# First attention of a fused block on Trainium2: the causal mask in 32-row matmuls, projections split around the last flips, weights loaded in another order

## The chip, the cores and the metric

The kernel runs on one core of one Trainium2 chip, as one launch. Its time is the device time of that core in microseconds. TensorE (PE) does the matmuls and transposes, VectorE (DVE), ScalarE (ACT) and GpSimd (POOL) the elementwise work. SyncE (SP) and POOL issue the DMAs.

## The reference, cut to what matters

A block over `x` of 8 batches x 128 positions x 512: a per-batch weight, a causal attention, a second attention with a paged cache, and a low-rank feed-forward. The change touches only the first two lines:

```python
h = einsum('bsi,boi->bso', x, weight[adapter_ids])       # one 512x512 weight per batch
q = (h @ wq)  # 32 heads of 16;   k, v = h @ wk, h @ wv   # 8 heads of 16, each for 4 query heads
scores = where(causal, q @ k.T * 0.25, lowest)
x = x + (softmax(scores) @ v) @ wo
x = x + ffn(attention_with_paged_cache(x))               # 32 heads of 128, untouched
```

## The kernel before, in words

The program is written in an order by hand: each engine executes its instructions in the order in which the code below emits them, and waits on semaphores where an operand is not ready. Tiles come from pools with a fixed number of buffers; a new tile waits until the oldest of its tag is free.

**Set-up.** SP's queue loads, in this order: `ids`, the first `x` (`load_x(0)`), `lens`, `freq`, `x1`, the weights of keys, values and queries of the first attention (`wk_sb`, `wv_sb` of 256 KB, `wq_sb` of 1 MB), four small page tables, the output weights (`wo_sb`, 1 MB), two more `x`, and small constants. SP has eight semaphores for these loads in turn, so a ninth load waits until the first has landed. POOL makes an identity and a causal mask, then gathers the weights of batch 0 and batch 1 from HBM (`gather_w`, four indirect DMAs of 256 KB each, rows given by `idx_w`).

**Per batch.** `flip_x` transposes `x` (PE, then a copy by ACT); `condition` multiplies with the gathered weights (`hp`, L498) and a copy makes `hT`; `project_kv` and `project_q` give keys, values and queries; `keep_k`, `keep_v` (ACT) and `keep_q` (DVE) move them out of PSUM.

**Per half-batch k (16 of them), 16 query heads.** `scores1` fills four PSUM banks j. First the mask goes in (L562): for each bank a matmul of the identity (weights, 128x128 bf16) with the mask (128x512 bf16). Then the products of queries and keys are added (L572): for each bank two matmuls that use only 32 of the 128 rows, rows 32j to 32j+31. DVE takes the maxima (`nm`), ACT the exponentials (`exps1`), DVE the sums and POOL the division (`divide1`). In the *next* step, `flip_p` transposes the probabilities in four portions j (PE, L615), each copied out as `pT` by DVE or ACT, and `values1` (L634) multiplies them with the values. `p_tp`, the PSUM pool of all transposes, has two buffers, and so has `p_mm`, that of the projections and products.

The main loop interleaves these. In even k: scores, `condition` of the next batch, flips 0 and 1 of the last step, divisions, keys and values of the next batch, flips 2 and 3 (copied by ACT), `values1`. In odd k: scores, output projection `out_proj1` of the batch before (L650), flips 0 and 1, divisions, queries of the next batch, flips 2 (ACT) and 3 (DVE), `flip_x`, `values1`. After the 16 half-batches come 64 units of the second attention and the feed-forward, where the change touches nothing.

Of the kernel before, what the change touches and what calls it, by code (L numbers as in the profile page):

```python
# [10 lines left out]

F32 = mybir.dt.float32
BF16 = mybir.dt.bfloat16
# [6 lines left out]
P = 128  # L20
# [21 lines left out]
def block_kernel(  # L42
# [47 lines left out]
    def tile_a(shape, name):  # L90
        return both.tile(shape, F32, tag="a", name=name, bufs=12)
# [184 lines left out]
    with (  # L276
# [9 lines left out]
        def load_x(b):  # L286
            if b < B:
                xss[b] = p1.tile([P, DM], F32, tag="xs", name=f"xs_{b}", bufs=4)
                nc.sync.dma_start(out=xss[b][:], in_=x[b])

        def gather_w(b):
            if b < B:
# [30 lines left out]
        ]  # L323
        for v in vpad:
            nc.vector.memset(v[:], 0.0)
        identb = p1w.tile([P, P], BF16, tag="identb", name="identb")
        nc.vector.tensor_copy(identb[:], ident[:])
        causal_f = both.tile([P, P], F32, tag="ka", name="causal_f")
        make_causal_mask(nc, causal_f[:], NEG)
        causal = p1w.tile([P, 4, P], BF16, tag="causal", name="causal")  # L330
        for n in range(4):
            nc.vector.tensor_copy(causal[:, n, :], causal_f[:])
        for c in range(KC):
            nc.vector.tensor_scalar(
                idx_w[:, c, :], ids[:], float(DM), iota_pf[:, c : c + 1], ALU.mult, ALU.add
            )
        gather_w(0)
        load_x(1)
        for sb, src in ((wk_sb, wk1), (wv_sb, wv1), (wq_sb, wq1)):
            nc.sync.dma_start(out=sb[:], in_=src.rearrange("(c p) e -> p c e", p=P))  # L340
        gather_w(1)

        pages = p1w.tile([P, B * NBLK], I32, tag="pages", name="pages")
        for n in range(4):
            nc.sync.dma_start(
                out=pages[n * PSIZE : (n + 1) * PSIZE, :],
                in_=table[n : n + 1].rearrange("n b k -> n (b k)").to_broadcast([PSIZE, B * NBLK]),
            )
        nc.sync.dma_start(out=wo_sb[:], in_=wo1.rearrange("(r p) e -> p r e", p=P))
        load_x(2)  # L350
        load_x(3)
        wn = [both.tile([P, D2], F32, tag="kb", name=f"wn_{n}") for n in range(2)]
        nc.sync.dma_start(out=wn[0][:], in_=qn_w.unsqueeze(0).to_broadcast([P, D2]))
        nc.sync.dma_start(out=wn[1][:], in_=kn_w.unsqueeze(0).to_broadcast([P, D2]))
# [17 lines left out]
        def angles():  # L372

            fr = p1.tile([P, B, D2 // 2], F32, tag="pT", name="ang_f", bufs=5)
            kf = p1.tile([P, B, D2 // 2], F32, tag="pT", name="ang_k", bufs=5)

            for n, key in enumerate(("sin", "cos")):
                trig[key] = x1T[B - 1 - n][:].rearrange("p c (h d) -> p (c h) d", d=HALF)
            pos = p1.tile([P, B], F32, tag="pos", name="pos", bufs=1)
            nc.vector.tensor_copy(lens_f[:], lens[:])  # L380
            nc.vector.tensor_scalar(pos[:], lens_f[:], iota_pf[:, :1], None, ALU.add)
            for b in range(B):
                nc.vector.tensor_scalar(fr[:, b, :], freq[:], pos[:, b : b + 1], None, ALU.mult)
            nc.vector.tensor_scalar(kf[:], fr[:], 1.0 / (2 * PI), ROUND, ALU.mult, ALU.add)
            nc.vector.tensor_scalar(kf[:], kf[:], ROUND, None, ALU.subtract)
            for part in (TWO_PI_1, TWO_PI_2, TWO_PI_3):
                nc.vector.scalar_tensor_tensor(fr[:], kf[:], -part, fr[:], ALU.mult, ALU.add)
            nc.vector.tensor_scalar(kf[:], fr[:], PI / 2, -2 * PI, ALU.is_gt, ALU.mult)
            nc.vector.scalar_tensor_tensor(kf[:], fr[:], PI / 2, kf[:], ALU.add, ALU.add)
            for a, t in ((fr, trig["sin"]), (kf, trig["cos"])):  # L390
                nc.vector.tensor_scalar(a[:], a[:], PI_IN, -PI_IN, ALU.min, ALU.max)
                nc.scalar.activation(t, a[:], AF.Sin)

        def tables(n):
            for here, there in ((lo, hi), (hi, lo)):
# [95 lines left out]
        def condition(b):  # L491
            hp = p_mm.tile([P, KC, S], F32, tag="mm", name=f"hp_{b}")
            parts = [(oc, c) for oc in range(KC) for c in range(KC)]
            if b == 0:

                parts.sort(key=lambda part: part[1])
            for n, (oc, c) in enumerate(parts):
                nc.tensor.matmul(  # L498
                    hp[:, oc, :],
                    cws[b][c][:, oc * P : (oc + 1) * P],  # L500
                    xT[b][:, c, :],
                    start=(n == 0 if b == 0 else c == 0),
                    stop=(n == KC * KC - 1 if b == 0 else c == KC - 1),
                )
            hT[b] = both.tile([P, KC, S], F32, tag="vg", name=f"hT_{b}", bufs=4)
            nc.vector.tensor_copy(hT[b][:], hp[:])

        def project_q(b):
            ps = p_mm.tile([P, REP, S], F32, tag="mm", name=f"qp1_{b}")
            for r in range(REP):  # L510
                for c in range(KC):
                    nc.tensor.matmul(  # L512
                        ps[:, r, :],
                        wq_sb[:, c, r * P : (r + 1) * P],
                        hT[b][:, c, :],
                        start=(c == 0),
                        stop=(c == KC - 1),
                    )
            return ps

        def keep_q(b, ps):
            qT[b] = p1.tile([P, REP, S], F32, tag="qT1", name=f"qT1_{b}")
            nc.vector.tensor_scalar(qT[b][:], ps[:], SCALE1, None, ALU.mult)

        def project_kv(b):
            ps = p_mm.tile([P, 2, P], F32, tag="mm", name=f"kvp1_{b}")
            for c in range(KC):
                nc.tensor.matmul(
                    ps[:, 0, :], wk_sb[:, c, :], hT[b][:, c, :], start=(c == 0), stop=(c == KC - 1)
                )  # L530
            for c in range(KC):
                nc.tensor.matmul(
                    ps[:, 1, :], hT[b][:, c, :], wv_sb[:, c, :], start=(c == 0), stop=(c == KC - 1)
                )
            return ps

        def keep_k(b, ps):
            kbd[b] = p1.tile([P, 2, S], F32, tag="kbd", name=f"kbd_{b}")
# [16 lines left out]
        def scores1(k):  # L555
            b, hb = divmod(k, 2)
            h = H[k]
            h["sc"] = [
                p_sc.tile([P, 2, 4 * S], F32, tag="sc", name=f"sc1_{k}_{n}") for n in range(2)
            ]  # L560
            for j in range(4):
                nc.tensor.matmul(  # L562
                    h["sc"][j // 2][:, j % 2, :],
                    identb[:],
                    causal[:].rearrange("p n t -> p (n t)"),
                    start=True,
                    stop=False,
                )
            for rr in range(2):
                for j in range(4):  # L570
                    rows = slice(32 * j, 32 * j + 32)
                    nc.tensor.matmul(  # L572
                        h["sc"][j // 2][:, j % 2, rr * 2 * S : (rr + 1) * 2 * S],
                        qT[b][rows, 2 * hb + rr, :],
                        kbd[b][rows].rearrange("p h t -> p (h t)"),
                        start=False,
                        stop=(rr == 1),
                    )
            h["nm"] = p1.tile([P, 2, 8], F32, tag="nm1", name=f"nm1_{k}")
            for n in range(2):  # L580
                nc.vector.tensor_reduce(
                    h["nm"][:, n, :],
                    h["sc"][n][:].rearrange("p j (h t) -> p (j h) t", t=S),
                    AX.X,
                    ALU.max,
                    negate=True,
                )
            h["pr"] = []
# [72 lines left out]
        by_vector, by_scalar = nc.vector.tensor_copy, nc.scalar.copy  # L661

        flip_x(0)
        angles()
        condition(0)
        flip_x(1)
        kv = project_kv(0)
        keep_k(0, kv)
        keep_v(0, kv)
        keep_q(0, project_q(0))  # L670
        gather_w(2)

        for k in range(2 * B + 1):
# [4 lines left out]
            if hb == 0:  # L678
# [17 lines left out]
                    divide1(k, 0)  # L696
                    divide1(k, 1)
                if more:
                    kv = project_kv(b + 1)
                if k == 2 * B:  # L700
                    merge_b(0)
                if k:
                    flip_p(last, 2, by_scalar)
                    flip_p(last, 3, by_scalar)
                if more:
                    keep_k(b + 1, kv)
                if k == 2 * B:
                    merge_b(1)
# [9 lines left out]
            else:  # L718
# [6 lines left out]
                divide1(k, 0)  # L725
                divide1(k, 1)
                if more:
                    ps = project_q(b + 1)
                    keep_q(b + 1, ps)
                else:  # L730
                    for c in range(KC):
                        q_matmul(0, c)
                    for part in q_turn(0):
                        part()
                    for c in range(KC):
                        kv_matmul(0, c)
                flip_p(last, 2, by_scalar)
                flip_p(last, 3, by_vector)
                if not more:
                    kv_turn(0)  # L740
                    norms(0)
                if b + 2 < B:
# [360 lines left out]
```

## Time and profile before

| | us |
|---|---|
| median of 3 runs (1441.12 to 1443.71) | 1442.05 |
| the profiled execution, its time | 1443.16 |
| the profiled execution, its span | 1441.4 |
| PE busy in the span | 1404.8 (97%) |
| DVE, ACT, POOL busy | 932.7, 652.6, 564.3 |
| first attention, mask matmuls (L562), first to last start | 25.8 to 207.0 |
| one pair of half-batches (58.83 to 83.41) | 24.58 |

Busy time of PE is the union of its matmuls, whose ends are modelled; a matmul that has been started counts as busy although the next one may already be waiting. About a quarter of the mask's records (16 of 64) are missing from the trace. The distance between the starts of two groups is therefore the safer reading than the busy time of one.

### The profile page before, as it was taken

The numbers are of one execution on the slowest core, as the hardware profiler recorded it, in microseconds if no ns is written. First come the engines' busy times: TensorE is split into PE (matmuls) and PEld (weight loads), VectorE is DVE, ScalarE is ACT, GpSimd is POOL, SyncE is SP. The second block draws the span as 40 slices with busy tenths as digits, with TensorE's granted clock in tenths as the row PEclk, the third lists the DMA queues.
The fourth block names the chain that finished last, engine by engine and source line by source line (L and its number), as shares of the span: only waits on it lengthen the run. The fifth ranks groups of instructions, "written<-read, shape, count | busy, mean of one in ns | idle before, by whom it ended". The sixth has DMA issues, their size and how long they took to land.

```text
span 1441.4 us, 19823 instructions
## 1 busy us (share of the span) xinstructions
PE 1404.8 (97%) x5984; PEld 897.3 (62%) x6000; DVE 932.7 (65%) x2271; ACT 652.6 (45%) x1513; POOL 564.3 (39%) x546
## 2 busy tenths in 40 slices
PE   6999999899999999999999999999999999999997
PEld 5677764566666666666666666666666665666554
DVE  4666674666666666666666666666666665666652
ACT  3454543444444444444444444444444444344430
POOL 4675242433333333333433344444343333343220
PEclk9999999999999999999999999999999999999999
DMA  5233410444444575444445654444457544444442
GB/s 202 75 117 120 142 44 23 134 120 118 117 117 117 150 191 159 118 117 117 118 119 160 194 149 119 119 119 119 119 161 193 157 125 136 123 115 114 112 111 66
DMA packets 159770, 181.82 MB, mean 126 GB/s; under 512 B 94960, under 2 KB 100336, under 8 KB 159664
## 3 DMA queue, kind: packets, MB, share of 16 engines
q1 hardware_dynamic: 144816, 138.59, 34.1%
q0 software_dynamic: 14848, 41.96, 10.4%
q8 instruction: 49, 0.80, 0.2%
q14 instruction: 57, 0.47, 0.1%
HBM read 75.57 MB, written 4.72 MB: 56 GB/s over the span
## 4 chain that ended last, share of the span: by engine, by line
PE 92%; SPq 2%; DMA 2%; DVE 2%; issue 1%; ACT 1%; POOL 0%; DVEq 0%; POOLq 0%
PE op L894 18%; PE qp L175 15%; PE sc L838 15%; PE yp L913 15%; PE kvp L215 7%; PE sc L845 4%; PE hp L498 2%; PE att L650 2%; PE qTp L252 2%; PE qp L512 2%; PE fp L960 2%; PE pT1p L615 2%; PE o L634 2%; SPq L882 1%; PE sc L572 1%; PE sc L562 1%
## 5 line engine op out<-in xcount | busy, mean ns | idle before, releaser
L851 DVE CUSTOM_DVE_ANT_0 pr<-sc,mask,nq 128x640 f32<-128x640 f32 x256 | 225.8, 883 | 142.2 <-PE sc L845 130.1
L861 ACT ACTIVATE pr<-pr,nm 128x640 f32<-128x640 f32 x256 | 211.8, 827 | 188.8 <-DVE nm L851 185.9
L838 PE MATMUL sc<-kT,qT 128*128 128x512 f32 x512 | 263.8, 597 | 2.2 <-DMA pT<-fl 1.8
L175 PE MATMUL qp<-wq,x1T 128*128 128x512 f32 x512 | 251.2, 593 | 0.0
L894 PE MATMUL op<-pT,vg 128*128 128x256 f32 x1024 | 243.4, 381 | 4.7 <-DMA pT<-fl 4.3
L913 PE MATMUL yp<-wo,oT 128*128 128x512 f32 x512 | 231.0, 594 | 0.0
L201 POOL TENSOR_TENSOR qa<-qa,qb 128x512 f32<-128x512 f32 x64 | 81.6, 1276 | 371.9 <-DVE sums L828 371.9
L894 PEld LDWEIGHTS op<-pT,vg 128*128 128x128 f32 x1024 | 194.7, 191 | 32.4 <-issue 4.1
L829 ACT ACTIVATE pr<-pr,sums 128x640 f32<-128x640 f32 x256 | 208.4, 814 | 0.0
L832 DVE STREAM_TRANSPOSE fl<-pr 128x640 f32<-128x640 f32 x256 | 192.2, 807 | 0.8 <-DMA kT<-flk 0.6
L845 PEld LDWEIGHTS sc<-kTo,qT 128*128 128x128 f32 x512 | 97.0, 190 | 125.3 <-issue 104.4
L913 PEld LDWEIGHTS yp<-wo,oT 128*128 128x128 f32 x512 | 92.3, 190 | 93.3 <-issue 91.8
L158 POOL DMA_INDIRECT kg<-in_k_cache_dram,idx_kv x128 | 132.1, 1032 | 35.3 <-issue 34.9
L158 POOL DMA_INDIRECT vg<-in_v_cache_dram,idx_kv x128 | 128.2, 1002 | 36.7 <-issue 33.9
L838 PEld LDWEIGHTS sc<-kT,qT 128*128 128x128 f32 x512 | 88.1, 192 | 82.2 <-issue 78.6
L254 ACT COPY qT<-qTp 128x512 f32<-128x512 f32 x64 | 37.5, 586 | 205.8 <-PE qTp L252 205.8
L215 PEld LDWEIGHTS kvp<-wkv,x1T 128*128 128x128 f32 x512 | 97.3, 190 | 40.5 <-issue 30.1
L215 PE MATMUL kvp<-wkv,x1T 128*128 128x256 f32 x512 | 120.9, 379 | 0.0
L242 POOL TENSOR_TENSOR rs<-ss,minus_half 128x5 f32<-128x5 f32 x64 | 76.6, 1197 | 82.3 <-DVE ss L240 82.3
L175 PEld LDWEIGHTS qp<-wq,x1T 128*128 128x128 f32 x512 | 82.8, 191 | 31.5 <-issue 31.5
L845 PE MATMUL sc<-kTo,qT 128*128 128x128 f32 x512 | 99.3, 276 | 0.0
L606 POOL TENSOR_TENSOR pr<-pr,sums 128x1024 f32<-128x1024 f32 x32 | 60.0, 1898 | 92.6 <-DVE sums L605 89.7
(134 smaller groups left out, 1645.6 us busy)
## 6 DMA issues: line engine op xcount, KB each, us to landing
pT<-fl SPq DMA_DIRECT2D x1024, 80.0 KB
kT<-flk SPq DMA_DIRECT2D x496, 32.0 KB
wq<-in_wq_dram SPq DMA_DIRECT2D x8, 1024.0 KB
wo<-in_wo_dram SPq DMA_DIRECT2D x8, 1024.0 KB
wkv<-in_wkv_dram SPq DMA_DIRECT2D x8, 512.0 KB
xs<-in_x_dram SPq DMA_DIRECT2D x8, 256.0 KB
x_kept<-x SPq DMA_DIRECT2D x8, 256.0 KB
kg<-in_k_cache_dram,idx_kv POOLq DMA_INDIRECT x128, 3.6
```

The source lines that it names most:

```text
L158: nc.gpsimd.indirect_dma_start(out=dst[:, c].rearrange("p n d -> p (n d)"), out_offset=None, in_=src, in_offset=bass.IndirectOffsetOnAxis( ...
L175: nc.tensor.matmul(s["qp"][:].rearrange("p h d -> p (h d)"), x1T[b][:, c, :], weights[g][0][:, c, :], start=(c == 0), stop=(c == KC - 1),)
L201: nc.gpsimd.tensor_tensor(qa[:], qa[:], qb[:], ALU.add)
L215: nc.tensor.matmul(s["kp"][:], x1T[b][:, c, :], weights[g][1][:, c, :], start=(c == 0), stop=(c == KC - 1))
L829: nc.scalar.activation(prs[r][:], prs[r][:], AF.Copy, scale=sums[:, r : r + 1])
L832: nc.vector.transpose(s["flips"][:, :, :, r, :].rearrange("p b c j -> p c b j"), prs[r][:])
L838: nc.tensor.matmul(sc[:, : NBLK * P].rearrange("p (k j) -> p k j", j=32), s["qT"][:, r, :], s["kT"], start=True, stop=True,)
L845: nc.tensor.matmul(sc[:, NBLK * P : NK], s["qT"][:, r, :], s["kTo"][:], start=True, stop=True)
L851: nc.vector.tensor_tensor_reduce(out=pr[:], in0=sc[:, :NK], in1=mask[:], scale=s["nq"][:, r : r + 1], scalar=3.0e38, op0=ALU.add, op1=ALU.min,
L861: nc.scalar.activation(pr[:], pr[:], AF.Exp, bias=nm[:, r : r + 1], scale=-1.0, accum_out=sums[:, r : r + 1],)
L894: nc.tensor.matmul(ops[h][:, : 2 * S], cached(u, "vg", c) if c < NBLK else s["vo"][:], s["pT"][:, :, c, 2 * h : 2 * h + 2, :].rearrange("p ...
L913: nc.tensor.matmul(yp[:], s["oT"][:, r, :], weights[g][2][:, r, :], start=(r == 0), stop=(r == REP - 1))
```

## The change

It has three parts.

1. **Mask.** `causal` is now laid out as four tiles of 32 rows, one copy for each row group j, and is the *weights* of the matmul; the moving operand is `eye32`, an identity of 32, four times side by side. For each bank j and each quarter c of the positions a matmul of 32 rows, 128 weights' columns and 4x32 moving columns writes columns 32c to 32c+31 of four heads: 16 matmuls in place of 4. `eye32` and `causal` are made by VectorE and by POOL's iotas instead of `make_causal_mask`.
2. **Order in the loop.** `project_kv` is split into `project_k` and `project_v`, and flips 2 and 3 stand between them. `project_q` is split: three heads ahead of flips 2 and 3, the fourth behind them, and `keep_q` behind that. At the start, the two sines stand behind `keep_v`, and the first `hT` is copied by ACT.
3. **Loads.** `wq_sb` and the second `x` are issued on SP behind the page tables. `wo_sb` and the third and fourth `x` are issued on POOL, behind the gathers for batches 0 and 1.

```diff
@@ load_x
-                nc.sync.dma_start(out=xss[b][:], in_=x[b])
+                queue = nc.gpsimd if b in (2, 3) else nc.sync
+                queue.dma_start(out=xss[b][:], in_=x[b])
@@ set-up
-        identb = p1w.tile([P, P], BF16, tag="identb", name="identb")
-        nc.vector.tensor_copy(identb[:], ident[:])
-        causal_f = both.tile([P, P], F32, tag="ka", name="causal_f")
-        make_causal_mask(nc, causal_f[:], NEG)
-        causal = p1w.tile([P, 4, P], BF16, tag="causal", name="causal")
-        for n in range(4):
-            nc.vector.tensor_copy(causal[:, n, :], causal_f[:])
         for c in range(KC):
             nc.vector.tensor_scalar(
                 idx_w[:, c, :], ids[:], float(DM), iota_pf[:, c : c + 1], ALU.mult, ALU.add
             )
+        eye_f = p1w.tile([P, 32], F32, tag="eye_f", name="eye_f")
+        nc.vector.tensor_reduce(
+            eye_f[:], ident[:].rearrange("p (n r) -> p r n", r=32), AX.X, ALU.add
+        )
+        eye32 = p1w.tile([P, 4, 32], BF16, tag="eye32", name="eye32")
+        nc.vector.tensor_copy(eye32[:], eye_f[:].unsqueeze(1).to_broadcast([P, 4, 32]))
+        row = p1w.tile([P, 1], I32, tag="row", name="row")
+        for n in range(4):
+            nc.gpsimd.iota(
+                row[32 * n : 32 * n + 32, :], pattern=[[0, 1]], base=0, channel_multiplier=1
+            )
+        row_f = p1w.tile([P, 1], F32, tag="row_f", name="row_f")
+        nc.vector.tensor_copy(row_f[:], row[:])
+        ahead = both.tile([P, 4, P], I32, tag="a", name="ahead", bufs=12)
+        nc.gpsimd.iota(ahead[:], pattern=[[-32, 4], [1, P]], base=0, channel_multiplier=0)
+        ahead_f = tile_a([P, 4, P], "ahead_f")
+        nc.vector.tensor_copy(ahead_f[:], ahead[:])
+        causal = p1w.tile([P, 4, P], BF16, tag="causal", name="causal")
+        nc.vector.tensor_scalar(causal[:], ahead_f[:], row_f[:], NEG, ALU.is_lt, ALU.mult)
         gather_w(0)
-        load_x(1)
-        for sb, src in ((wk_sb, wk1), (wv_sb, wv1), (wq_sb, wq1)):
+        gather_w(1)
+        nc.gpsimd.dma_start(out=wo_sb[:], in_=wo1.rearrange("(r p) e -> p r e", p=P))
+        load_x(2)
+        load_x(3)
+        for sb, src in ((wk_sb, wk1), (wv_sb, wv1)):
             nc.sync.dma_start(out=sb[:], in_=src.rearrange("(c p) e -> p c e", p=P))
-        gather_w(1)
...
-        nc.sync.dma_start(out=wo_sb[:], in_=wo1.rearrange("(r p) e -> p r e", p=P))
-        load_x(2)
-        load_x(3)
+        load_x(1)
+        nc.sync.dma_start(out=wq_sb[:], in_=wq1.rearrange("(c p) e -> p c e", p=P))
@@ scores1
-            for j in range(4):
-                nc.tensor.matmul(
-                    h["sc"][j // 2][:, j % 2, :],
-                    identb[:],
-                    causal[:].rearrange("p n t -> p (n t)"),
-                    start=True,
-                    stop=False,
-                )
+            for c in range(4):
+                for j in range(4):
+                    rows = slice(32 * j, 32 * j + 32)
+                    nc.tensor.matmul(
+                        h["sc"][j // 2][:, j % 2, :].rearrange("p (n t) -> p n t", n=4)[
+                            :, :, 32 * c : 32 * c + 32
+                        ],
+                        causal[rows, c, :],
+                        eye32[rows],
+                        start=(c == 0),
+                        stop=False,
+                    )
@@ condition
-            nc.vector.tensor_copy(hT[b][:], hp[:])
+            (nc.vector.tensor_copy if b else nc.scalar.copy)(hT[b][:], hp[:])
@@ before the loop
-        kv = project_kv(0)
+        kv = project_k(0)
+        project_v(0, kv)
         keep_k(0, kv)
         keep_v(0, kv)
-        keep_q(0, project_q(0))
+        for a, t in turns:
+            nc.scalar.activation(t, a[:], AF.Sin)
+        ps = new_q(0)
+        project_q(0, ps, range(REP))
+        keep_q(0, ps)
@@ loop, even k
                 if more:
-                    kv = project_kv(b + 1)
+                    kv = project_k(b + 1)
...
                 if k:
                     flip_p(last, 2, by_scalar)
                     flip_p(last, 3, by_scalar)
                 if more:
+                    project_v(b + 1, kv)
                     keep_k(b + 1, kv)
@@ loop, odd k
                 if more:
-                    ps = project_q(b + 1)
-                    keep_q(b + 1, ps)
+                    ps = new_q(b + 1)
+                    project_q(b + 1, ps, range(REP - 1))
...
                 flip_p(last, 2, by_scalar)
                 flip_p(last, 3, by_vector)
-                if not more:
+                if more:
+                    project_q(b + 1, ps, (REP - 1,))
+                    keep_q(b + 1, ps)
+                else:
                     kv_turn(0)
                     norms(0)
```

More of the change, by code (lines that the diff above doesn't have):

```diff
@@ L9 @@
 from concourse._compat import with_exitstack
-from concourse.masks import make_causal_mask, make_identity
+from concourse.masks import make_identity
 F32 = mybir.dt.float32
@@ L389, in angles @@
             nc.vector.scalar_tensor_tensor(kf[:], fr[:], PI / 2, kf[:], ALU.add, ALU.add)
-            for a, t in ((fr, trig["sin"]), (kf, trig["cos"])):
+            for a in (fr, kf):
                 nc.vector.tensor_scalar(a[:], a[:], PI_IN, -PI_IN, ALU.min, ALU.max)
-                nc.scalar.activation(t, a[:], AF.Sin)
+            return (fr, trig["sin"]), (kf, trig["cos"])
         def tables(n):
@@ L505, in condition, with new_q, project_q @@
             hT[b] = both.tile([P, KC, S], F32, tag="vg", name=f"hT_{b}", bufs=4)
-            nc.vector.tensor_copy(hT[b][:], hp[:])
-        def project_q(b):
-            ps = p_mm.tile([P, REP, S], F32, tag="mm", name=f"qp1_{b}")
-            for r in range(REP):
+            (nc.vector.tensor_copy if b else nc.scalar.copy)(hT[b][:], hp[:])
+        def new_q(b):
+            return p_mm.tile([P, REP, S], F32, tag="mm", name=f"qp1_{b}")
+        def project_q(b, ps, heads):
+            for r in heads:
                 for c in range(KC):
@@ L518, in project_q @@
                     )
-            return ps
         def keep_q(b, ps):
@@ L523, in keep_q, with project_k @@
             nc.vector.tensor_scalar(qT[b][:], ps[:], SCALE1, None, ALU.mult)
-        def project_kv(b):
+        def project_k(b):
             ps = p_mm.tile([P, 2, P], F32, tag="mm", name=f"kvp1_{b}")
@@ L530, in project_kv, with project_v @@
                 )
+            return ps
+        def project_v(b, ps):
             for c in range(KC):
@@ L534, in project_kv @@
                 )
-            return ps
         def keep_k(b, ps):
@@ L663, in block_kernel @@
         flip_x(0)
-        angles()
+        turns = angles()
         condition(0)
         flip_x(1)
-        kv = project_kv(0)
+        kv = project_k(0)
+        project_v(0, kv)
         keep_k(0, kv)
         keep_v(0, kv)
-        keep_q(0, project_q(0))
+        for a, t in turns:
[3 more added lines that the diff above has]
+        keep_q(0, ps)
         gather_w(2)
```

## The prediction

> **What bounds the kernel now.** I read the page first (its chain, then its groups), then the first 270 us group by group with shapes kept apart, then the order of time on TensorE, on ScalarE and on the DMA queues. The page's chain:
>
> ```profile
> PE 92%; SPq 2%; DMA 2%; DVE 2%; issue 1%; ACT 1%; POOL 0%; DVEq 0%; POOLq 0%
> ```
>
> TensorE carries 92% of the path from end to start, and the changed stage (the first attention, about 0 to 215 us) is no exception. So time taken off TensorE there, be it work or a hole, comes off the end; work moved between other engines counts only where TensorE waits for it. The groups of 0 to 270 us (columns: busy us, mean ns of one | idle before):
>
> ```profile
> L634 PE MATMUL o<-pT,vpad 128*32 128x256 f32 x256 | 25.0, 388 | 1.2 <-DVE pT L621 1.2
> L572 PE MATMUL sc<-kbd,qT 32*128 32x256 f32 x256 | 18.3, 400 | 0.0
> L562 PE MATMUL sc<-causal,identb 128*128 128x512 bf16 x48 | 13.1, 379 | 2.3 <-issue 2.2
> ```
>
> L562 is the mask: 4 matmuls for each of 16 half-batches k (16 of 64 records are missing). Look at L572: 256 matmuls of 400 ns each would fill 102 us, but the engine is busy 18.3 us with them. Four matmuls on four groups of 32 rows run abreast. L562's do not: they use all 128 rows and follow each other. One pair of half-batches on TensorE (start, us):
>
> ```profile
> 76.73 1.16 PE L528 MATMUL kvp<-hT,wk_sb 128*128 128x128 f32 x8
> 77.73 1.06 PE L532 MATMUL kvp<-wv_sb,hT 128*128 128x128 f32 x8
> 78.62 1.04 PE L615 MATMUL pT1p<-ident,pr 128*128 128x128 f32 x8
> 79.59 1.85 PE L634 MATMUL o<-pT,vpad 128*32 128x256 f32 x16
> ...
> 91.40 1.04 PE L615 MATMUL pT1p<-ident,pr 128*128 128x128 f32 x8
> 92.68 0.66 PE L483 MATMUL xTp<-ident,xs 128*128 128x128 f32 x4 [0.24 <-ACT pT L621]
> 93.26 1.07 PE L634 MATMUL o<-pT,vpad 128*32 128x256 f32 x16
> ```
>
> The same 16 records of L634 take 1.85 us in the even step and 1.07 in the odd one. The even one stands directly behind the last flips (L615), and two of its four inputs must still be copied by ScalarE:
>
> ```profile
> 79.26 1.08 ACT L621 COPY pT<-pT1p 128x512 f32<-128x512 f32 x2 [1.86 <-PE pT1p L615]
> ```
>
> The copies end at 80.34, so 0.78 us of the 1.85 is waiting, though the row shows no idle time (the four matmuls in hand overlap it). In the odd step the wait stands before xTp: the flips start at 91.40 and need about 0.88 us, xTp starts at 92.68, so 0.4 us is lost. The chain in order of time gives the mask's place on the path:
>
> ```profile
> 81.44 0.16 issue
> 81.60 0.81 PE sc L562 x3
> 82.41 1.08 PE sc L572 x16
> 83.49 3.63 PE att L650 x8
> ```
>
> The mask costs 0.16 + 0.81 = 0.97 us per step. Last, the start:
>
> ```profile
> 4.14 1.17 POOL L295 DMA_INDIRECT cw<-in_cond_w_dram,idx_w  x1 [1.41 <-DVE idx_w L334]
> 12.73 6.56 PE L498 MATMUL hp<-xT,cw 128*128 128x128 f32 x32 [7.26 <-DMA cw<-in_cond_w_dram,idx_w]
> 27.65 3.84 PE L498 MATMUL hp<-xT,cw 128*128 128x128 f32 x32
> ```
>
> The first product waits 7.26 us for the first gather, and then needs 6.56 us where the same 32 records later need 3.84.
>
> ```profile
> DMA  0343699999999999600000000067840000000000
> ```
>
> This is 0 to 60 us in slices of 1.5: the DMA engines are full from 7.5 to 24 us.
>
> **The change part by part.**
>
> A. The mask. 4 matmuls with 512 columns become 16 of 32 rows with 128 columns, each with its own weights, four on four row groups and four PSUM banks at a time. Array time of one with 512 columns: the three recorded span 0.81 us with the 0.379 that one takes, so they start 0.215 apart; 128 columns are a quarter, 0.054. If four run abreast as L572's do, four rounds are 0.22 us. I add 0.1 us for loading weights and entering the mode: 0.32. The scores behind it then use the same 32-row split, so no change of mode lies between. Saved: 0.97 - 0.32 = 0.65 a step, times 16 = 10.4 us. The weight loads (16, not 4) are new in this form: L562's own take 98 ns each, L572's 184, and those of L572 hide behind the round before. Bounds: 0.2 us (rounds with nothing between, 12.3 saved) and 16 pairs in strict sequence, 98 + 54 = 0.15 us each, 2.4 us (23 lost).
>
> Here the skill speaks against the change. The Trainium skill, "TensorE: Matmul & The Clock Gate", section "Back-to-back issue gap", gives about 81 ns per matmul for a sustained stream of weight load and matmul pairs with 128 columns. 16 x 81 = 1.30 us (estimate from that page), against 0.97 now: 0.33 lost a step, 5.3 us in all. The row of L572 is nearer: its 16 pairs, with 256 columns in two passes, take 1.08 us on the chain, that is 67 ns a pair where the array alone needs 0.215 us for each. They could not do so if pairs on different row groups queued for each other. [...]I take the trace's 0.32 and keep 81 ns a pair as a rival.
>
> B. The projections. In even steps (k = 2 to 12, six of them) the values' projection, 0.89 us (21.23 to 22.13 on the chain at the start), moves between the last flips and L634. ScalarE's two copies end 0.75 us after L634 now starts, so the projection covers them: 0.78 x 6 = 4.7 us. What is late next: keep_k waits behind the copies as before, and the queue of ScalarE is free by then (exponentials end at 77.4, the flips come at about 77.6 instead of 78.5). In odd steps (k = 3 to 13, six) one head of queries, 16 of 64 records or 0.89 us, moves between the flips and xTp and covers the 0.4 us: 2.4 us. keep_q is now behind the last pT copy on VectorE; it ends about 0.7 us after the fourth head, and its reader, the scores, is 0.4 (xTp) + 1.0 (L634) + 0.3 (mask) away. In step 1 everything hangs on exponentials, sums, then qT (0.64 us) and only then pT on VectorE; pT now goes first: 0.6 us. Sum of B 7.7. Bounds: 0 if the copies get later by as much, and 8.5.
>
> C. The start. Ahead of the first gathers only the small loads, the first x and the keys' and values' weights stay on SP; the 1 MB of queries' weights goes behind the page tables and x1, where its queue waits for freq (landed at 7.6, where the fourth page table is issued). The 1 MB of output weights, x2 and x3 go to POOL's queue behind the second set of gathers. The first gather's issue at 4.14 stays (it hangs on ids). It lands at 12.6 now; a later gather in a quiet time lands 4.0 us after issue, which would be 8.1. But wk, wv and x1 still fill the queues until about 9, so I take 10.4, the middle: hp starts 2.2 us sooner. It stays slow: the Trainium skill, same page, part 1 (the clock gate), says that an idle engine runs at half clock until it was busy for a window of about 3.4 us. The granted clock of the page reads full here, so it does not show this; the 6.56 against 3.84 us does, with 26 starts 0.213 us apart and then 0.11. Without the rule one could hope for 2.7 us more by early gathers; with it hp keeps its 6.56. hT by ScalarE takes 0.59, not 0.69: 0.1. Queries' weights are asked for 4 us later; they landed at 16.2 (SP's next issue waited for them), and are needed at 22.0 - 2.3 = 19.7, so even a shift of the whole 4 us costs only 0.5. C is 2.3; bounds 4.6 and -1.
>
> What is costed at nothing: VectorE's new set-up (a reduction of 0.37, three small casts, two passes over 128x512 of 0.43 each, about 1.6 us) is behind idx_w and fits into its 2.85 us idle before ang_f. POOL's five iotas (four of 0.16, one of 0.57; the mask's two of 0.5 fall away) fit into the 1.41 us that POOL waits before its first gather. POOL's three plain DMAs (a gather costs 0.95 to 1.17 us of POOL; 4 times as many rows in the output weights, so 3 to 6 us for all) and their waits for earlier landings push the third set of gathers from 14.7 to about 20; the next POOL work comes at 33.7, after 14.37 us idle, and those gathers are read at 47.5. Without that cover they would delay the divisions. The two sines move behind keep_v: table load 1.28, sines 1.24, table load 1.28 end at about 24.3, before the first exponential's input at about 26.
>
> Sum: 10.4 + 7.7 + 2.3 = 20.4 us off the profiled execution's 1443.16, which gives 1422.8; that execution is 1.1 above the median of 1442.05, so 1421.7 for the median. A shorter first stage shifts the rest as it stands: later waits follow TensorE.
>
> **The rivals.**
>
> R1. The mask's pairs do not run abreast and cost the page's 81 ns: A is -5.3, the sum 4.7, 1437.4. For it: weight loads are now as many as matmuls and each matmul is short, and no row has this shape. Against: L572.
>
> R2. The start gains nothing, because the gathers are slow for reasons of their own (the first bytes come late also while the DMA engines are only three to six tenths busy): C is 0 to -1, 1424 to 1425. For it: wk, wv and x1 are the same bytes before 9 us.
>
> R3, slower than before. Mask pairs run in strict sequence with their weight loads exposed, in the place of L562: 0.15 us a pair, 2.4 us a step, 22.9 lost, B and C give back 10.0: 1455. It decides from 10.0/16 = 0.63 us above 0.97, that is 1.6 us a step or 100 ns a pair. For it: output runs of 32 columns and loads of 98 ns, both untried here. Against: in L572 loads of the next round start with the matmuls of this one.
>
> R4. The cover fails: ScalarE's or POOL's chain is late when TensorE arrives sooner, and B's waits reopen before the flips: B is 2 at most, 1427.4. For it: exponentials of one step end only 1.1 us before the flips are copied. Against: POOL's divisions end 3.4 us before their flips.
>
> **How the numbers follow.** The forecast's case has 0.65, R1 0.10, R2 0.11, R4 0.07, R3 0.07. The point is the first case's 1421.7. Its best bounds (12.3 + 8.5 + 4.6 = 25.4) end at 1416.7; upward, a mask at 0.6 us (5.9 saved) with C at nothing gives 1428.5 and R4 with a weak mask 1432. I give 1416 to 1433; R1 and R3 lie outside. Faster by over 0.2% (2.9 us, what a measurement here can tell from no change) is all but R3 and the tail of R1: 0.90; same 0.03; slower 0.07.
>
> **What would show it.** Right: the mask's group takes 0.25 to 0.45 us from its first start to the scores' and no longer 0.97; L634 takes 1.0 to 1.1 us in even steps too; xTp follows without a hole; hp starts at about 10.4, still some 6.5 us long; a pair of steps is 22.1 us, not 24.6. Wrong: matmuls of the mask start 80 ns apart or more (R1, R3), hp starts at 12 or TensorE waits for wq_sb (R2), or it waits before L615 for POOL's division (R4).

## The result, and the profile after

| | before | after |
|---|---|---|
| median, on one chip (4 runs each) | 1441.59 us | 1423.46 us (1422.94 to 1425.07) |
| the profiled execution | 1443.16 us, span 1441.4 | 1425.07 us, span 1423.3 |

The ratio is 0.9874 (95% interval 0.986 to 0.9889): 18.1 us, or 1.3%, faster. 1421.7 had been forecast, 20.4 us less. The two profiled executions lie 1.6 us above their medians and differ by the same 18.1 us. The page's chain:

```profile
PE 91%; SPq 3%; DVE 2%; issue 2%; DMA 1%; POOL 1%; ACT 1%; DVEq 0%; POOLq 0%; ACTq 0%
```

TensorE still carries the path. The groups of 0 to 270 us, shapes kept apart (busy us, mean ns of one | idle before):

```profile
L658 PE MATMUL o<-pT,vpad 128*32 128x256 f32 x256 | 20.2, 386 | 1.2 <-DVE pT L645 1.2
L596 PE MATMUL sc<-kbd,qT 32*128 32x256 f32 x256 | 17.5, 389 | 0.5 <-DVE qT L541 0.5
L584 PE MATMUL sc<-eye,causal 32*128 32x128 bf16 x256 | 6.4, 217 | 0.0
```

The values' products (L658, was L634) are the same 256 records of about the same length, but busy 20.2 us and not 25.0: what is gone is waiting that had been counted as busy. The mask (L584) has 256 records of 217 ns, 55.6 us if they followed each other, in 6.4 us of busy time. The pair of half-batches that the prediction showed, now on TensorE (start, us):

```profile
70.93 1.16 PE L546 MATMUL kvp<-hT,wk_sb 128*128 128x128 f32 x8
71.93 1.04 PE L639 MATMUL pT1p<-ident,pr 128*128 128x128 f32 x8
72.80 1.06 PE L553 MATMUL kvp<-wv_sb,hT 128*128 128x128 f32 x8
73.79 1.07 PE L658 MATMUL o<-pT,vpad 128*32 128x256 f32 x16
74.79 0.40 PE L584 MATMUL sc<-eye,causal 32*128 32x128 bf16 x16
75.02 1.09 PE L596 MATMUL sc<-kbd,qT 32*128 32x256 f32 x16
...
83.13 1.04 PE L639 MATMUL pT1p<-ident,pr 128*128 128x128 f32 x8
84.00 1.06 PE L531 MATMUL qp<-hT,wq_sb 128*128 128x128 f32 x8
84.90 0.60 PE L500 MATMUL xTp<-ident,xs 128*128 128x128 f32 x4
85.43 1.07 PE L658 MATMUL o<-pT,vpad 128*32 128x256 f32 x16
```

The reader is to see three distances between starts. Mask to scores: 74.79 to 75.02, where the mask had taken 0.97. L658 to the mask in the even step: 1.00 us (was 1.78 on the chain of before, 79.66 to 81.44). xTp follows the fourth head of queries without a hole (was 0.4). A pair of steps, mask 53.02 to mask 74.79, takes 21.77 us instead of 24.58.

The start, from the order of time of all engines, and below it the DMA engines' busy tenths of 0 to 60 us in slices of 1.5:

```profile
6.54 0.38 SPq L368 DMA_DIRECT2D wq_sb<-in_wq_dram  x1
8.56 0.74 SPq L372 DMA_DIRECT2D bias<-in_ffn_b_dram  x1
9.68 3.75 PE L515 MATMUL hp<-xT,cw 128*128 128x128 f32 x16 [4.17 <-DMA cw<-in_cond_w_dram,idx_w]
14.83 3.54 PE L515 MATMUL hp<-xT,cw 128*128 128x128 f32 x16 [1.39 <-DMA cw<-in_cond_w_dram,idx_w]
```

```profile
DMA  0344999999999999970000000476600000000045
```

The first product starts 3.05 us sooner (9.68, was 12.73), but stops half way for the third gather and ends at 18.37 (was 19.29). The queries' products start at 20.93 (was 21.96): 1.03 us of the 3.05 are left.

**Where the 18.1 us come from.** By the first starts of the same groups in both traces (for the mask those of its weight loads, since matmul records of before are missing): 0.83 us at the first mask; 17.4 more from the first to the fifteenth; 0.8 in each of the last two steps; 0.5 in the first units of the second attention. There after is 20.3 us ahead, and stays so for 47 units. Then 2.1 us are lost: 0.5 at unit 48, where TensorE waits 1.65 us for POOL's `qa` and had waited 1.15; 0.4 at unit 62; and 1.2 in the last 20 matmuls of L927, which span 7.02 us from first to last start (before: 5.86). Before these 20 both kernels wait alike for `pT` (3.31 us before, 3.38 after), but then the granted clock is at half for 6.8 us in after, and for 3.4 in before. The rows are windows of the two profiles, after's first: from and to, the length, the busy us and instructions of PE, PEld, DVE, ACT and POOL, the granted clock, the DMA share and GB/s:

```profile
1400.40:1407.20 6.80, 5.76 (x14) 4.62 (x15) 0.42 (x1) 0.00 (x0) 1.26 (x1) 0.50 0.38 117
```

```profile
1421.40:1424.80 3.40, 3.40 (x10) 2.69 (x9) 0.00 (x0) 0.00 (x0) 1.26 (x1) 0.50 0.43 145
1424.90:1431.00 6.10, 5.60 (x18) 3.08 (x17) 1.31 (x3) 0.00 (x0) 0.00 (x0) 1.00 0.00 0
```

A like stretch at half clock, at the first units of the second attention, is 3.4 us long in after and 6.8 in before, so the 0.5 gained there may come from the clock as well.

One loss is inside the stage. Step 13 should have gained like the other odd steps (1.25), but gained 0.34: its L658 group takes 2.28 us. On VectorE, the first product of the gates' merge is four to five times too long:

```profile
160.66 3.75 POOL L630 TENSOR_TENSOR pr<-pr,sums 128x1024 f32<-128x1024 f32 x2 [8.42 <-DVE sums L629]
162.72 2.98 DVE L448 TENSOR_TENSOR gs<-gc,sel 128x256 f32<-128x256 f32 x4
```

```profile
L448 DVE TENSOR_TENSOR gs<-gc,sel x4: 412/412/1972, 162.7 to 165.3; 128x256 f32<-128x256 f32 x4
```

```profile
L431 DVE TENSOR_TENSOR gs<-gc,sel x4: 411/412/1219, 180.6 to 182.4; 128x256 f32<-128x256 f32 x4
```

The first fence is the order of time, the second the view of the tile `gs` (minimum/median/maximum ns), the third the same view in before. POOL divides until 164.41; the first of the four products starts at 162.72, takes 1.97 us instead of 0.41, and ends at 164.69. Before had this hold too, only shorter: POOL divided until 181.51, the first product started at 180.57 and took 1.22 us. The maxima of step 13 (`nm`), which stand behind it on VectorE, then the exponentials, sums and `pT` are late by as much.

### The profile page after: what moved, and what is told of

It reads as the page before. It is cut to its first block, busy times and chain, and to the rows that moved or that the text cites. A ratio compares the mean times of both kernels' runs of the same rounds, so it can differ in the third digit from the quotient of the medians.

```text
span 1423.3 us, 20224 instructions
## 1 busy us (share of the span) xinstructions
PE 1390.3 (98%) x6192; PEld 895.2 (63%) x6192; DVE 935.1 (66%) x2270; ACT 653.3 (46%) x1514; POOL 566.7 (40%) x552
## 4 chain that ended last, share of the span: by engine, by line
PE 91%; SPq 3%; DVE 2%; issue 2%; DMA 1%; POOL 1%; ACT 1%; DVEq 0%; POOLq 0%; ACTq 0%
PE op L927 19%; PE qp L175 15%; PE sc L871 15%; PE yp L946 15%; PE kvp L215 7%; PE sc L878 4%; PE hp L515 2%; SPq L915 2%; PE qTp L252 2%; PE att L674 2%; PE fp L993 2%; PE pT1p L639 2%; PE qp L531 2%; PE o L658 1%; PE sc L596 1%
## 5 line engine op out<-in xcount | busy, mean ns | idle before, releaser
L927 PE MATMUL op<-pT,vg 128*128 128x256 f32 x1024 | 244.6, 382 | 5.6 <-DMA pT<-fl 5.6
L927 PEld LDWEIGHTS op<-pT,vg 128*128 128x128 f32 x1024 | 195.6, 192 | 33.6 <-issue 5.4
L273 ACT COPY kTo<-kTp 128x128 f32<-128x128 f32 x64 | 17.1, 267 | 167.3 <-PE kTp L271 167.3
```

Of the source, the lines that this page charges most:

```text
L927: nc.tensor.matmul(ops[h][:, : 2 * S], cached(u, "vg", c) if c < NBLK else s["vo"][:], s["pT"][:, :, c, 2 * h : 2 * h + 2, :].rearrange("p ...
```

## The experiments

The kernels were timed in three groups, each on one chip with runs of the kernel before beside them: e_mask to e_rowseq and after_again to e_gates on chip 6, after_third to best3 on chip 9. The medians of before differ by up to 9 us between chips, so only ratios, or kernels of one group, are compared.

| kernel | median us | before, same group | ratio, 95% interval |
|---|---|---|---|
| e_mask | 1439.42 | 1449.80 | 0.993 [0.9903, 0.9956] |
| e_split | 1440.77 | 1449.80 | 0.9927 [0.99, 0.9953] |
| e_loads | 1445.08 | 1449.80 | 0.9969 [0.9957, 0.9981] |
| e_rowseq | 1428.52 | 1449.80 | 0.9847 [0.982, 0.9874] |
| after_again | 1431.94 | 1450.42 | 0.9876 [0.9861, 0.9892] |
| e_fullrow | 1439.52 | 1450.42 | 0.9925 [0.9911, 0.9938] |
| e_wq_warm | 1429.38 | 1450.42 | 0.9863 [0.9847, 0.9879] |
| e_gates | 1427.31 | 1450.42 | 0.9844 [0.9831, 0.9858] |
| after_third | 1424.46 | 1443.44 | 0.9873 [0.9855, 0.989] |
| e_bcast | 1424.39 | 1443.44 | 0.987 [0.9854, 0.9885] |
| e_bcast_wq | 1421.06 | 1443.44 | 0.9844 [0.983, 0.9858] |
| best3 | 1420.04 | 1443.44 | 0.9841 [0.9827, 0.9854] |

### One part alone: e_mask, e_split, e_loads

The kernel before, each with one part of the change: the mask's set-up and its 16 matmuls; the split projections; the order of loads at the start.

```diff
 e_mask:  causal, eye32 and scores1 as after, all else as before
 e_split: project_k / flips 2, 3 / project_v, and 3 + 1 heads of queries, all else as before
 e_loads: wq_sb, x1, wo_sb, x2, x3, gather_w(1), sines, first hT as after, all else as before
```

> The kernel before with only the mask changed (16 matmuls of 32 rows, and the set-up that makes their operands). Theory 'the parts add up': the trace after shows mask and scores together in 1.25 us from the mask's first start to the next group where before it was 2.05, so 0.79 us in 15 of 16 steps less up to 0.4 us for entering the 32-row mode from the full array in steps 0 and 1: 11 to 12 us faster, about 1430. Rival 'the flips' copies set the pace': with a shorter mask TensorE only arrives sooner at the copies it waits for, the holes in front of L634 and xTp grow, and the gain stays under 7 us, about 1435. Rival 'pairs of 81 ns': 5 us slower, 1447.

> The kernel before with only the projections split around the last flips. Theory 'the parts add up': 0.78 us in six even steps, 0.4 in six odd steps, about 0.6 in step 1, and 0.3 or so lost again in step 13: 6.5 to 7.5 us faster, about 1434.5. Rival 'the cover is used up': under 3 us, if the copies are late for another reason than the flips (ScalarE still in the exponentials).

> The kernel before with only the start changed (order and queues of the loads, sines behind keep_v, first hT by ScalarE). Theory: hp starts at about 9.7 instead of 12.7 but stops after 16 records for the third gather, which lands at 14.8 as before; the first score follows about 1.0 us sooner; 0.8 to 1.2 us faster, about 1440.5. Rival 'the prediction's 2.3 us': the loss against it came from the mask's new operands on VectorE and POOL, then this kernel gains 2 us or more.

Measured: 10.4, 9.0 and 4.7 us less than before. In the trace of e_mask each of the steps 2 to 12 is 0.79 us shorter than in before's; step 1 gains 0.89, step 13 0.5, and step 0 nothing: with the short mask its scores wait 0.54 us for `qT`, which the long mask had covered. In that of e_split the even steps gain 0.78, the odd ones 0.46, and step 1 0.60. So both mechanisms hold, at the size forecast or a little above it. The mask alone changes nothing at L650 (the values' products there); with the projections split, e_split's L637 no longer waits:

```profile
78.41 1.85 PE L650 MATMUL o<-pT,vpad 128*32 128x256 f32 x16
80.19 0.40 PE L576 MATMUL sc<-eye,causal 32*128 32x128 bf16 x16
```

```profile
80.22 1.06 PE L536 MATMUL kvp<-wv_sb,hT 128*128 128x128 f32 x8
81.21 1.07 PE L637 MATMUL o<-pT,vpad 128*32 128x256 f32 x16
```

e_loads gained 4.7 where 0.8 to 1.2 had been expected. With the old order of loads the queries' products start at 21.96 (before), 23.84 (e_mask) and 24.98 us (e_split), with the new one at 20.93 (after), 18.87 (e_loads) and 19.09 (e_rowseq); the means of these three and three differ by 4.0. Two things spread them that are not the landing of a gather. The first product turns from starts 0.213 us apart to about 0.11 at a moment that differs from trace to trace: 18.5 in before, 18.0 in after, 12.8 in e_loads. And in e_mask and e_split the copy of the first product waits until 21.2, though the product ends at 19.75 and 17.96; ScalarE's copy beside it waits as long. In order of time, e_split:

```profile
12.79 5.17 PE L498 MATMUL hp<-xT,cw 128*128 128x128 f32 x32 [7.37 <-DMA cw<-in_cond_w_dram,idx_w]
21.16 0.69 DVE L506 COPY hT<-hp 128x512 f32<-128x512 f32 x1 [6.81 <-remote]
```

What holds both engines there the traces do not name. The trace of before, from another group, does not have it, and no trace with the new order has it. So the gain of the start is 1.0 us in one pair of traces and 4.7 in the medians of chip 6, and how much of it is the order of the loads stays open. The three gains together (24.1) are more than after's 18 to 19, within what their intervals leave open.

### What makes 16 small matmuls cheap: e_rowseq, e_fullrow

```diff
 e_rowseq
-            for c in range(4):
-                for j in range(4):
+            for j in range(4):
+                for c in range(4):
 e_fullrow: 128 rows each, weights one causal block of 128 x 128, moving 32 columns of the identity x 4
-                        causal[rows, c, :],
-                        eye32[rows],
+                        causal[:],
+                        eyes[:, c],
```

> The changed kernel with the mask's two loops exchanged: the same 16 matmuls, but the four of one row group follow each other and then comes the next group. Theory 'four row groups abreast': the rounds are gone, each matmul follows its predecessor in the same rows after 56 ns, with overlap only where the group changes: the mask takes 0.7 to 0.9 us in place of 0.24, 16 x 0.5 to 0.65 = 8 to 10.5 us slower than the changed kernel, about 1432 to 1434. Rival 'a stream of pairs costs 81 ns in one tile': 1.3 us for the mask, 17 us slower, about 1440. Rival 'it is the shorter columns and the one mode for mask and scores that gain, not the rows side by side': no difference, 1423.

> The mask again in 16 matmuls of 128 columns, each with its own weights, but each over all 128 rows (one causal block of 128 x 128 as weights, one of four selections of 32 columns as the moving input), so that no two can run on different row groups. If the row groups are what makes 16 pairs cheap, the mask costs 16 x 0.056 = 0.9 us a step or more instead of 0.24: about 0.7 us x 15 = 10 us slower than the changed kernel, as slow as the kernel before the mask was changed. If a weight load and matmul pair of 128 columns costs 81 ns (the rival), 16 x 0.081 = 1.3 us: 16 us slower. If short outputs or anything else but the row groups made it cheap, it equals the changed kernel.

Two lines of each trace, e_rowseq first, then e_fullrow:

```profile
73.12 0.43 PE L584 MATMUL sc<-eye,causal 32*128 32x128 bf16 x16
73.35 1.12 PE L596 MATMUL sc<-kbd,qT 32*128 32x256 f32 x16
```

```profile
78.48 1.07 PE L576 MATMUL sc<-eyes,causal 128*128 128x128 bf16 x16
79.48 1.15 PE L588 MATMUL sc<-kbd,qT 32*128 32x256 f32 x16
```

With the four row groups one after another in program order, mask to scores is still 0.23 us, and a step is only 0.03 us longer: the expectation that the interleaving matters missed. The 16 matmuls start about 14 ns apart on average; the records do not say which rows each one is on, so whether four of one group really start so close, or the engine takes the groups in turn, is not shown. With all 128 rows the same number of matmuls of the same length takes 1.00 us, 62 ns a pair of weight load and matmul (starts 56 ns apart, then 0.15 us to the first score), and 7.6 us of the gain are gone (1439.52 against 1431.94; 9.7 by the traces, over the 14 steps to the fifteenth mask). So it is the row groups that pay, neither the short moving operand nor the number of columns written. Without them the new form costs what the old one did (1.00 against 0.97).

### The start: e_wq_warm, e_bcast, e_bcast_wq

```diff
 e_wq_warm, e_bcast_wq
         gather_w(0)
+        nc.gpsimd.dma_start(out=wq_sb[:], in_=wq1.rearrange("(c p) e -> p c e", p=P))
         gather_w(1)
...
-        nc.sync.dma_start(out=wq_sb[:], in_=wq1.rearrange("(c p) e -> p c e", p=P))
 e_wq_warm only, between the flips of the first x and the first product
+        for n in range(10):
+            nc.tensor.matmul(idle[:, 0, :P], ident[:], ident[:], start=True, stop=True)
 e_bcast, e_bcast_wq: behind x3 on POOL's queue
-        nc.sync.dma_start(out=wn[0][:], in_=qn_w.unsqueeze(0).to_broadcast([P, D2]))
+        nc.gpsimd.dma_start(out=wn[0][:], in_=qn_w.unsqueeze(0).to_broadcast([P, D2]))
 (wn[1] and bias alike)
```

> Two additions at the start. The queries' weights (1 MB) are asked for on POOL's queue right behind the first gathers, not on SP ahead of the third gather, so that the gathers are not held by them; and ten fp32 matmuls of the identity, into a score tile that nothing reads, are put on TensorE between the flips of the first x and the first condition product, to keep it busy. If the first product is bound by the clock and by the third gather together, the product ends at about 15 to 16 us instead of 18.2, and the whole is 2 to 3 us shorter. If it is bound by the landings of the third and fourth gather alone (14.8 and 15.6), which share the DMA engines with everything else, it ends at about 16.5 and gains at most 1.5. If queries' weights become late, TensorE waits for them instead, and nothing is gained.

> Only the three loads that spread one row over 128 partitions (the two norm weights and the bias) are moved from SP, where the changed kernel asks for them at 7.4 to 9.3 us, to POOL's queue behind x3. In the kernel before they stood behind the queries' weights' landing, at 16.2 us; the change brought them into the time of the first gathers, and their packets take the engines' time without many bytes (in the run with the queries' weights moved, the DMA engines were 0.9 busy at 160 GB/s between 10 and 14 us). If they are what makes the third gather late (14.4 to 14.8 us), it lands at 12 to 13, the first product ends 1 to 2 us sooner and the whole gains as much. If the queries' weights or the gathers themselves are, the third gather still lands at 14 or later and nothing is gained: the same within 1 us.

> The same, and the queries' weights on POOL's queue right behind the first four gathers. If the gathers are held by both, the four land by about 11 to 12 us, the first product (started at 9.7, slow until TensorE was busy for a few us) ends at about 14 to 15, not 18, and the first mask starts at about 21, 3 us sooner than in the changed kernel. If the gathers are slow for reasons of their own (the rival R2 of the prediction), the third still lands at 14 or later, and the gain is under 1 us.

e_wq_warm differs from its partner after_again by less than their intervals tell apart, and its first mask is later (26.02 against 24.39 us). TensorE in order of time:

```profile
5.35 3.54 PE L691 MATMUL idle<-ident 128*128 128x128 f32 x20
9.80 1.13 PE L515 MATMUL hp<-xT,cw 128*128 128x128 f32 x8 [0.91 <-issue]
11.19 1.16 PE L515 MATMUL hp<-xT,cw 128*128 128x128 f32 x8 [0.26 <-DMA cw<-in_cond_w_dram,idx_w]
14.67 4.30 PE L515 MATMUL hp<-xT,cw 128*128 128x128 f32 x16 [2.32 <-DMA cw<-in_cond_w_dram,idx_w]
```

Kept busy beforehand, TensorE does the first 16 records in 1.13 + 1.16 us, where after needs 3.75: the slow first product is a matter of what TensorE did before it. But nothing is won, for two reasons. The third gather lands at 14.6 as before, though the queries' weights no longer stand ahead of it. And from 14.56 to 21.38 the granted clock is at half again, after 3.4 us in which TensorE was busy for 1.16; the last 16 records take 4.30 us:

```profile
11.15:14.56 3.41, 1.16 (x8) 0.97 (x8) 2.00 (x4) 0.00 (x0) 2.50 (x4) 1.00 0.84 166
14.60:21.30 6.70, 6.49 (x27) 5.97 (x28) 0.00 (x0) 1.17 (x2) 3.80 (x6) 0.50 1.00 382
```

The DMA queues of this trace between 10 and 14 us (packets, MB, share of 16 engines):

```profile
q1 hardware_dynamic: 330, 0.28, 60.2%
q0 software_dynamic: 111, 0.37, 27.9%
```

SP's queue (q1) has by then, from the order of its issues, little but the three loads that spread one row over 128 partitions, the two norm weights and the bias. For 0.28 MB they hold the engines more than twice as long as the gathers (q0) do for 0.37. In the kernel before they were issued at 16.2 us, behind the landing of the queries' weights. The change frees SP, and so issues them at 7.4 to 9.3, among the gathers.

e_bcast moves these three alone, and is the same as after_third: now the queries' weights keep the engines, and from 10 to 12 us SP's queue has 95.5% of them and POOL's 8.5%. e_bcast_wq moves both, and there between 10 and 14 us POOL's queue has the engines to itself:

```profile
q0 software_dynamic: 367, 1.35, 96.4%
q1 hardware_dynamic: 19, 0.03, 1.9%
```

Its first product, from the order of time, no longer stops:

```profile
9.31 6.08 PE L515 MATMUL hp<-xT,cw 128*128 128x128 f32 x32 [3.81 <-DMA cw<-in_cond_w_dram,idx_w]
```

The queries' products start at 17.96 us, against 19.45 in after_third and 20.63 in e_bcast, and the time is 3.4 us under after_third's (1421.06 and 1424.46; the intervals of the ratios overlap at their edges only). So the gathers were held by both loads in turn, and taking one away let the other in. Not all of the difference between these traces is that: the clock turned full at 14.1 us in e_bcast_wq, at 15.6 in after_third and only at 19.1 in e_bcast, and how much of the 3.4 us the clock made was not separated.

### The hold on VectorE, and all together: e_gates, best3

```diff
 e_gates
-                if k == 2 * B - 4:
-                    merge_gates()
                 ...
+                if k == 2 * B - 3:
+                    merge_gates()
 best3 = e_bcast_wq + e_gates
```

> The gates' merge (four products of 128 x 256 on VectorE) is issued one step later, behind the scores of the last pair and not beside POOL's division of the step before. In the changed kernel the first of these four takes 1.97 us instead of 0.41 and ends 0.3 us behind the division, and the sums and copies behind it on VectorE come late: the last step's o group took 2.28 us, not 1.0. If the hold by POOL is the cause, the four take 0.41 each and 1.0 to 1.4 us of TensorE's waiting go. If the wait is only passed on (the merge has to be done before the second attention, and other work of VectorE stands behind it), the difference is under 0.5 us.

> All three: norm weights and bias behind x3, the queries' weights behind the first gathers, the gates' merge one step later. If the gains add, the run is 2 us (gates by their trace) to 4.6 us (gates by the medians) plus 1 to 3 us (start) faster than the changed kernel: about 0.984 of the kernel before, or less. If the waits behind it (the merge of the first output columns, DVE's late copies at about 180 us) take up the start's gain, it is no faster than the gates alone, 0.984 to 0.985.

The tile's view of e_gates:

```profile
L448 DVE TENSOR_TENSOR gs<-gc,sel x4: 418/418/424, 166.1 to 167.1; 128x256 f32<-128x256 f32 x4
```

Away from the division, all four products take 0.42 us, so the hold comes with POOL's work beside it. The twelve traces that have the merge beside the division, before's among them, agree: in each the first product ends 0.28 us behind the division. In after, VectorE's sums (1.2 us) and its copies of `o` (0.42) beside such divisions keep their length. Step 13 to 14 is 0.94 us shorter than in after_again, just under the 1.0 to 1.4 of the theory. The medians give 4.6 us in this group, but best3 is only 1.0 us under e_bcast_wq. 0.8 of the 4.6 lies in a wait of step 14 for `pT`, first in after_again, then in after_third:

```profile
187.59 1.16 PE L639 MATMUL pT1p<-ident,pr 128*128 128x128 f32 x8 [3.76 <-DVE pT L645]
```

```profile
182.98 1.16 PE L639 MATMUL pT1p<-ident,pr 128*128 128x128 f32 x8 [0.44 <-DVE pT L645]
```

On chip 6 seven of the eight traces wait 2.3 to 3.8 us there (in e_mask TensorE is held elsewhere in the same step, which takes 18.1 us and not 13.8); the four of chip 9 and the pair of the result wait 0.44. So this wait goes with the chip or the group, not with the kernel. What delays VectorE's copies there was not tried, and the rest of the 4.6 stays open.

best3 is the fastest of all: 4.4 us under after_third (1420.04, 1424.46), its queries' products start at 17.14. The gains add in part only: 3.4 for the start, 1.0 for the gates.

### The changed kernel again: after_again, after_third

> The changed kernel unaltered, beside the others of this call, so that their differences to it are taken on one chip. It also asks how far its own trace repeats. If the second gain at the start (first product from 9.7 to about 18.2 us, with 1.4 us of waiting for the third gather) is fixed by the program, hp again takes its 32 matmuls 0.213 us apart and ends at about 18. If it hangs on when the third gather lands and in which phase the clock gate is, the end of hp moves by 1 to 2 us with nothing changed. The last 20 matmuls of the output projection span either 5.9 or 7.0 us, by the same chance. Time: 0.987 of the kernel before.

> The changed kernel unaltered, as the partner of the others of this call on one chip. Its start shows once more how far the end of the first product (16.0 to 18.2 us in five traces so far) wanders by itself. Time 0.987 to 0.988 of the kernel before.

The ratio repeats: 0.9876 and 0.9873. The same program ends its first product at 18.16 and 16.88 us (first trace 18.37), and its last 20 matmuls of L927 span 5.86 us both times. The 1.2 us lost at the end of the first trace are thus not the change's. They go with the clock: after, e_split and e_fullrow, with 6.94 to 7.02 us there, have the clock at half for 6.8 us; the ten with 5.6 to 5.9 have it so for 3.4; and e_wq_warm, whose half clock came before these matmuls, takes 4.18.

## Why the prediction was right, and where it was off

- **A, the mask.** Right in its mechanism. Forecast 0.32 us a step, measured 0.234; saved 0.79 a step instead of 0.65. The term that was too large is the 0.1 us for loading weights and entering the mode: next to the 0.22 of the four rounds, 0.01 is left to see. That e_mask gave 10.4 us for a forecast of 10.4 is partly luck: a step saved more, but step 0 saved nothing. The trace of e_mask gives 10.1 over the first 14 steps.
- **R1 and R3, pairs in sequence.** Both fell. The Trainium skill's 81 ns a pair ("TensorE: Matmul & The Clock Gate", "Back-to-back issue gap") is for a stream of weight loads and matmuls, and that section names no row groups. On four row groups this case has 0.234/16 = 15 ns a pair, and even on all rows (e_fullrow) 62. Weighing the nearer row, L572, against the page was the right choice.
- **B, the projections.** Right: 7.7 forecast, 7.9 measured in e_split's trace over the first 14 steps. The even steps give 0.78, as said, the odd ones 0.46 for 0.4, step 1 0.60 as said. Not foreseen: with the projections split, VectorE comes to the gates' merge earlier in POOL's division and is held longer, 1.97 us and not 1.22, and step 13 loses 0.9 of its gain. It is R4's kind of loss, in one step of twelve, but on VectorE.
- **C, the start.** The start at 10.4 was 9.68, but the sum's second half failed: "hp keeps its 6.56". The product was split by the third gather and took 8.7 us, so that 3.05 us became 1.03 in this pair of traces. The prediction followed the first gather alone, and did not ask which other loads come sooner when SP is freed. The queries' weights were counted as 4 us later; SP's queue issued them at 6.54, 2.4 us later than before, still ahead of the third gather's data. The norm weights and the bias, which came 9 us sooner, were not counted at all. That the clock stays low at first was right, but for how long is not fixed: it turned full at 18.5 us in before and between 12.4 and 19.1 in the changed kernel and its variants without extra matmuls. R2, that the start gains nothing because the gathers are slow for reasons of their own, fell: the first one landed 3 us sooner, and in e_bcast_wq the others no longer held the product.
- **The sum.** 20.4 forecast; the two traces are 20.3 apart after the first unit of the second attention. "A shorter first stage shifts the rest as it stands" held for 47 units, and then failed by 0.9 us at two late waits and by 1.2 at the end, the latter by the longer half clock of that run. That the total came within 2.3 us of the forecast is in part luck: the mask gave more than its term and the start less, and 0.5 us gained and 1.2 lost go with the clock.
- **Costed at nothing.** The set-up on VectorE and POOL, the plain DMAs on POOL (0.84 us for the output weights, 1.14 for both x) and the sines stayed off the path: POOL still had 10 us of idle time before its first division.

## What to carry to other kernels

A matmul that can be written with 32 contraction rows can be worth splitting over TensorE's row groups, even if that makes four times as many matmuls and weight loads, as the mask here; judge it by starts in the trace of a neighbour with the same rows. A wait behind transposes costs nothing once independent matmuls stand in it, and the view to find it is the distance between starts, since a busy row hides it. When a queue is freed, list every load behind the one that moved: here the loads that spread a single row over all partitions took the engines' time with few bytes, and belonged behind whatever was waited for. And compare the granted clock of two traces before a late difference of a microsecond is put down to the change.

## What the runs showed of the hardware

- The order of the row groups in the program does not matter: four matmuls of one group, then four of the next, took the same 0.23 us as interleaved ones.
- A VectorE product of two SBUF tensors (fp32, 128x256) that met POOL's elementwise division ended 0.28 us behind the division in twelve traces out of twelve, and so took 1.22 or 1.97 us; moved away from it (e_gates, best3), 0.42.
- The granted clock at half is a slower TensorE: in e_wq_warm 0.50 from 14.56 to 21.38 us, with 16 records of the first product in 4.30 us; at full clock just before, 16 took 1.13 + 1.16.
- The 1.00 that the column shows during the slow first product of after is no measurement. The trace's records of the clock begin at 17.99 us (before: 18.51, e_split: 15.65, best3: 12.39), and what has no record is shown as 1.00; in each of these four traces the starts turn from 0.213 to about 0.11 us apart within 0.2 us of that moment.
